# Four-layer graph network: the norm through PSUM, a deeper lookahead, and GpSimd's sums as eight pointer-scalar adds

## The chip, the cores and the metric

The kernel runs on one core of a Trainium2 chip. Its engines are TensorE (PE in the profile; PEld is its weight load), VectorE (DVE), ScalarE (ACT), GpSimd (POOL) and SyncE (SP). The metric is the device time of one execution, in microseconds.

## The reference

The input x holds 64 graphs of 256 nodes with 128 features, and adj is one 256x256 matrix. Four layers follow each other; each adds the output of a graph layer to x, and each begins with a layer norm over the features and a Relu:

```python
h = jnp.maximum(_layernorm(x, axis=-1), 0.0)
x = x + layer(h, adj, weights)
```

Layer 0 is a gated recurrent unit of five steps (two sigmoids and a tanh on products of h and adj @ h). Layer 1 is a polynomial in adj with a Relu. Layer 2 is (adj + I) @ h through one weight, normalised to length one. Layer 3 is an attention whose score takes a leaky Relu of every pair of nodes:

```python
pre = s1[:, :, None, :] + s2[:, None, :, :] + b_lin   # (graph, i, j, 256 channels)
h = jnp.where(pre >= 0, pre, ALPHA * pre)
e = jnp.einsum('bije,e->bij', h, a) + bias
out = sigmoid(softmax(e, axis=2) @ x)
```

This last score is nearly all of the work: 64 graphs x 256 x 256 pairs x 256 channels.

## The kernel before

Work goes by pairs of graphs (NB = 2, 32 pairs). For a pair, `front(p)` (lines 314 to 446) computes layers 0 to 2 and the inputs of layer 3's score; it is a generator that hands control back at each `yield`, 85 pieces in all (STEPS_OF_FRONT). The score of a pair goes in 64 slots: slot n stands for a node block `ic` (two of 128 nodes) and a row r (32), and covers rows r, r+32, r+64 and r+96 of the block for both graphs. Each slot has two tiles of 128 partitions (channels) by 4 x 2 x 256 = 2048 values, one for each half of the channels:

- the first half, `rl_v` (L515), is one VectorE maximum of 128x2048 that reads `s2a` from PSUM and `s1n` from SBUF, both broadcast;
- the second half goes two ways. Of every three slots, two have GpSimd make the sum `rl_g` (L504 in `make_sum`: one broadcast tensor_tensor add of `s2b` and `s1b`, 128x2048, all in SBUF), and ScalarE then applies the Relu in place (L518). The third slot has ScalarE do sum and Relu at once in eight instructions of 128x256, with a column of `s1b` as the per-partition bias (L524, `rl_s`).

`scores(n)` (L527 to 536) then has TensorE multiply both tiles by a 128x32 window of weights, four row groups each, into the PSUM tile `pe`. After 32 slots a `tail` (L450 to 483) takes a block's scores through softmax, two matmuls and a tanh to the output; its last two GpSimd instructions are L480 (times 0.5 plus 0.5, 128x256) and L481.

The main loop (L567 to 583) writes out the order of the work. For slot n it issues make_sum(n + SUM_AHEAD), make(n + AHEAD), then some pieces of the front of the next pair and of the one after it (`advance`, by a count of yields), then on odd slots a piece of a tail, then scores(n). `in_order()` ties every instruction of TensorE, VectorE, ScalarE and GpSimd to the one before it on its engine, so each engine runs in exactly this program order. AHEAD is 2 and SUM_AHEAD 5; `rl_v` has 3 buffers, `rl_g` 4, `rl_s` 2. All short-lived PSUM tiles of fronts and tails rotate through five banks (`bank`).

A front calls `norm` (L236 to 255) four times: statistics on VectorE (L243, L245); `inverse_root` on GpSimd (L233 adds the epsilon, L234 raises to the power -0.5; it also serves layer 2's normalisation, on `rn`); then four VectorE tensor_scalar operations of 128x128 that subtract the mean and multiply, from SBUF into the SBUF tile `h` (L250); then GpSimd's maximum with zero over all of `h`, 128x512 (L254). The transposes of h by TensorE follow (L262), or products with adj (L278). L417, the layer 2 result, is a group of four VectorE operations of 128x128 that read PSUM and SBUF and write SBUF.

Of the kernel before, what the change touches and what calls it, by code (L numbers as in the profile page):

```python
# [14 lines left out]
P = 128  # L15
NB = 2
# [2 lines left out]
NORM_EPS = 1e-12  # L19
ALPHA = 0.2  # L20
ENGINES = (mybir.EngineType.PE, mybir.EngineType.DVE, mybir.EngineType.Activation, mybir.EngineType.Pool)
AHEAD = 2
SUM_AHEAD = 5
SLOTS = 64


# [1 line left out]
def kernel(  # L28
# [207 lines left out]
    def norm(src, h):  # L236

        stats = work.tile([P, NB * NC, 6], F32, name="stats")
        mv = work.tile([P, NB * NC, 2], F32, name="mv")
        s = src.rearrange("p b c d -> p (b c) d")  # L240
        hh = h.rearrange("p b c d -> p (b c) d")
        for k in range(NB * NC):
            nc.vector.bn_stats(stats[:, k, :], s[:, k, :])  # L243
        for k in range(NB * NC):
            nc.vector.bn_aggr(mv[:, k, :], stats[:, k, :])  # L245
        yield
        inverse_root(mv[:, :, 1], OP.add, LN_EPS)
        yield
        for k in range(NB * NC):
            nc.vector.tensor_scalar(hh[:, k, :], s[:, k, :], mv[:, k, 0:1], mv[:, k, 1:2],  # L250
                                    op0=OP.subtract, op1=OP.mult)
        yield
        hh = h.rearrange("p b c d -> p (b c d)")
        nc.gpsimd.tensor_scalar(hh, hh, 0.0, None, op0=OP.max)  # L254
        yield

    def to_feature(h, name):

# [42 lines left out]
    def feat(name, **kw):  # L301
        return work.tile([P, NB, N], F32, name=name, **kw)

    def tok(name, **kw):
        return work.tile([P, NB, NC, D], F32, name=name, **kw)

    def add_row(po, row):

        t = po.rearrange("p b c d -> p (b c) d")
        nc.vector.tensor_add(t, t, row.unsqueeze(1).to_broadcast([P, NB * NC, D]))  # L310
# [3 lines left out]
    def front(p):  # L314
# [1 line left out]
        x0 = XIN.pop(p)  # L316


        h = tok("h", bufs=3)
        yield from norm(x0, h)  # L320
        pt = to_feature(h, "pt")
        pm = mix_nodes(h, adj_t, "pm")
        yield
        hT = feat("hT", bufs=4)
        nc.scalar.copy(hT, pt)
        mT = feat("mT", bufs=3)
        nc.scalar.copy(mT, pm)
        yield
        for step in range(STEPS):
            if step:  # L330
                pm = mix_nodes(h, adj_t, "pm")
                yield
                mT = feat("mT", bufs=3)
                nc.scalar.copy(mT, pm)
                yield
            pr = project(bank([P, NB, N], "pr"), [(u3t, hT), (w4t, mT)])
            yield
            r = bank([P, NB, N], "r")
            nc.scalar.activation(r, pr, AF.Tanh, bias=br, scale=0.5)
            yield  # L340
            rh = feat("rh")
            nc.vector.scalar_tensor_tensor(rh, r, 1.0, hT, op0=OP.add, op1=OP.mult)
            project(pr, [(w34, mT)], start=False)
            yield
            nc.scalar.activation(pr, pr, AF.Tanh, bias=bz, scale=0.5)
            pv = project(bank([P, NB, N], "pv"), [(w5t, mT), (u5t, rh)])
            yield
            nc.scalar.activation(pv, pv, AF.Tanh, bias=bh, scale=1.0)  # L348
            yield

            d = feat("d")
            nc.vector.tensor_sub(d, pv, hT)
            nc.vector.scalar_tensor_tensor(pr, pr, 1.0, d, op0=OP.add, op1=OP.mult)  # L353
            hT_new = feat("hT", bufs=4)
            nc.vector.scalar_tensor_tensor(hT_new, pr, 0.5, hT, op0=OP.mult, op1=OP.add)  # L355
            hT = hT_new
            yield
            pt = to_token(hT, "pt")
            yield
            if step < STEPS - 1:  # L360
                h = tok("h", bufs=3)
                nc.scalar.copy(h, pt)  # L362
                yield
        x1 = tok("x1")
        nc.vector.tensor_add(x1, x0, pt)


        h = tok("h", bufs=3)
        yield from norm(x1, h)
        pt = to_feature(h, "pt")  # L370
        pm = mix_nodes(h, adj_n, "pm")
        yield
        hT = feat("hT", bufs=4)
        nc.scalar.copy(hT, pt)
        c1T = feat("c1T")
        nc.scalar.copy(c1T, pm)
        yield
        pt = to_token(c1T, "pt")
        yield
        c1 = tok("c1", bufs=1)  # L380
        nc.scalar.copy(c1, pt)
        yield
        pm = mix_nodes(c1, adj_n, "pm")
        yield
        c2T = feat("c2T", bufs=1)
        nc.vector.scalar_tensor_tensor(c2T, pm, 2.0, hT, op0=OP.mult, op1=OP.subtract)
        yield
        po = project_token([(hT, th[:, 0, :]), (c1T, th[:, 1, :]), (c2T, th[:, 2, :])], "po")
        yield
        add_row(po, bias1)  # L390
        x2 = tok("x2")
        nc.vector.scalar_tensor_tensor(x2, po, 0.0, x1, op0=OP.max, op1=OP.add)


        h = tok("h", bufs=3)
        yield from norm(x2, h)
        pm = mix_nodes(h, adj_ti, "pm")
        yield
        yT = feat("yT", bufs=1)
        nc.scalar.copy(yT, pm)  # L400
        yield
        po = project_token([(yT, w2)], "po")
        yield
        add_row(po, bias2)
        yield
        sq = tok("sq", bufs=1)
        nc.scalar.square(sq, po)
        yield
        rn = work.tile([P, NB * NC], F32, name="rn")
        nc.vector.tensor_reduce(rn, sq.rearrange("p b c d -> p (b c) d"), AX.X, OP.add)  # L410
        yield
        inverse_root(rn, OP.max, NORM_EPS * NORM_EPS)
        yield
        x3 = tok("x3")
        for b in range(NB):
            for c in range(NC):
# [4 lines left out]
        h3 = tok("h3")  # L421
        yield from norm(x3, h3)
        pt = to_feature(h3, "pt")
        yield
        hT = feat("hT3")
        nc.scalar.copy(hT, pt)
        yield
        p1 = project(bank([P, NB, N], "p1"), [(adj_t[:, 0, P:2 * P], hT)])
        p2 = project(bank([P, NB, N], "p2"), [(adj_t[:, 1, P:2 * P], hT)])
        yield  # L430
        s2b = feat("s2b")
        nc.scalar.copy(s2b, p2)
        s1b = feat("s1b")
# [2 lines left out]
        for k in range(NB * NC):  # L436
            b, c = divmod(k, NC)
            nc.tensor.matmul(pc[:, k:k + 1], hT[:, b, c * P:(c + 1) * P], g1, start=True, stop=True)
        yield
        crow = work.tile([P, NB * NC], F32, name="crow")  # L440
        nc.vector.tensor_scalar(crow, pc, c_b, None, op0=OP.add)
        p1 = project(bank([P, NB, N], "p1"), [(adj_t[:, 0, 0:P], hT)])
        yield
        s1n = feat("s1n")
        nc.scalar.activation(s1n, p1, AF.Identity, bias=nblin[:, 0:1], scale=-1.0)
        READY[p] = [x3, h3, hT, crow, s1n, s1b, None, s2b]

    STEPS_OF_FRONT = 85

    def tail(p, ic, pe, x3, h3, crow):  # L450

        t = work.tile([P, NB, N], F32, name="sc")
        for b in range(NB):
            nc.vector.scalar_tensor_tensor(t[:, b, :], pe[:, b, :], crow[:, b * NC + ic:b * NC + ic + 1], adj_n[:, ic, :],
                                           op0=OP.add, op1=OP.add)
# [9 lines left out]
        nc.vector.reciprocal(rs, sums)  # L465
        pt = to_token(t, "pt")
        yield
        wT = work.tile([P, NB, NC, P], F32, name="wT")
        nc.scalar.mul(wT, pt, 0.5)
        yield  # L470
        po = bank([P, NB, D], "po")
# [27 lines left out]
    def make_sum(n):  # L499
        if n >= NPAIR * SLOTS or n % 3 == 0:  # L500
            return
        ops = READY[where(n)[0]]
        TILES[n, 1] = relu_pool.tile([P, 4, NB, N], F32, name="rl_g", bufs=4)
        nc.gpsimd.tensor_add(TILES[n, 1], *operands(n, ops[5], ops[7]))  # L504

    def make(n):
        if n >= NPAIR * SLOTS:
            return
        p, ic, r = where(n)
        ops = READY[p]  # L510
        if ops[6] is None:
            ops[6] = ps_s.tile([P, NB, N], F32, name="s2a")
            project(ops[6], [(adj_t[:, 1, 0:P], ops[2])])
        TILES[n, 0] = relu_pool.tile([P, 4, NB, N], F32, name="rl_v", bufs=3)
        nc.vector.tensor_tensor(TILES[n, 0], *operands(n, ops[4], ops[6]), op=OP.max)  # L515
        if n % 3:
            t = TILES[n, 1].rearrange("p g b n -> p (g b n)")
            nc.scalar.activation(t, t, AF.Relu)  # L518
        else:
            TILES[n, 1] = relu_pool.tile([P, 4, NB, N], F32, name="rl_s", bufs=2)  # L520
            for g in range(4):
                for b in range(NB):
                    i = ic * P + g * 32 + r
                    nc.scalar.activation(TILES[n, 1][:, g, b, :], ops[7][:, b, :], AF.Relu,  # L524
                                         bias=ops[5][:, b, i:i + 1], scale=1.0)
# [13 lines left out]
    PE = [None]  # L539
    FRONTS = {}  # L540

    def advance(p, upto):

        if p >= NPAIR:
            return
        if p not in FRONTS:
            load_x(p + 1)
            FRONTS[p] = [front(p), 0]
        f = FRONTS[p]
        while f[1] < upto and p not in READY:  # L550
            next(f[0], None)
            f[1] += 1
            in_order()

    in_order()
    half = STEPS_OF_FRONT // 2
    for k in range(STEPS_OF_FRONT + 8):
        advance(0, k)
        advance(1, k * half // STEPS_OF_FRONT)
    for n in range(SUM_AHEAD):  # L560
        make_sum(n)
    for n in range(AHEAD):
# [4 lines left out]
    for n in range(NPAIR * SLOTS):  # L567
# [2 lines left out]
        make(n + AHEAD)  # L570
        in_order()
        k = min(n % SLOTS + 1, room)
        advance(p + 1, 10 ** 6 if k == room else half + k * (STEPS_OF_FRONT - half) // room)
        advance(p + 2, (n % SLOTS + 1) * half // SLOTS)
        if tails and n % 2:
            if next(tails[0], 0) == 0:
                tails.pop(0)
# [40 lines left out]
```

## Time and profile before

| | us |
|---|---|
| median of 3 runs | 6881.86 (6881.08 to 6882.07) |
| the profiled execution | 6881.12 |
| its span | 6879.3 |
| a pair of graphs in the steady state | about 210 |
| granted TensorE clock, mean | 0.933 |

A line of the groups of instructions reads: source line, engine, operation, output and inputs, shapes, count, then busy time in us and mean duration of one in ns, then the engine's idle time just before these instructions and what ended most of it. A line of a timeline reads: start, length, engine, source line, operation, operands, number of instructions, and in brackets the idle time before and what ended it. A tile's view gives the shortest, median and longest duration in ns, then the first and the last start. Durations of VectorE and ScalarE instructions overlap a little when they follow each other, so a group's time is less than count times duration.

### The profile page before, as it was taken

Reading aid. Unit: us, or ns where it says so; the run is one execution under the profiler, and the core shown is the slowest. Engines: PE = TensorE matmul, PEld = TensorE weight load, DVE = VectorE, ACT = ScalarE, POOL = GpSimd, SP = SyncE. Lnnn points to the kernel's source line nnn. Section 1 sums busy time; section 2 is a strip of 40 time slices with the busy share of each in tenths; the row PEclk is TensorE's granted clock in tenths of the full one; section 3 lists DMA queues with packets and bytes.
Section 4 is the critical chain, followed back from the end, with each engine's and each line's share of the span. In section 5 each row is a group of like instructions: output and inputs, shape, how many; then the busy total and the mean of one; then the engine's idle time right before and its main releaser. Section 6 shows DMA issues by size and latency. Waiting matters only on the chain.

```text
span 6879.3 us, 98866 instructions
## 1 busy us (share of the span) xinstructions
PE 5854.8 (85%) x40021; PEld 2128.4 (31%) x40021; DVE 6045.8 (88%) x4868; ACT 5442.0 (79%) x8366; POOL 5381.2 (78%) x1947
## 2 busy tenths in 40 slices
PE   6888888888888888888898888888888988888888
PEld 3333233322323333333233333233332333233222
DVE  3988998889889888988898888988889988888898
ACT  3787887878878787877887788877877877788789
POOL 2777787778878777877787788877877877787799
PEclk8999999999999999999999999999999999999999
DMA  0000000000000000000000000000000000000000
GB/s 14 3 3 4 4 2 4 3 4 4 2 4 4 3 4 2 4 4 3 4 4 2 4 3 4 4 2 4 3 4 4 2 4 4 3 2 2 2 3 3
DMA packets 38651, 24.43 MB, mean 4 GB/s; under 512 B 3504, under 2 KB 38192, under 8 KB 38192
## 3 DMA queue, kind: packets, MB, share of 16 engines
q1 hardware_dynamic: 35088, 17.05, 0.9%
q8 instruction: 313, 5.13, 0.3%
q10 hardware_dynamic: 3104, 1.05, 0.1%
q14 instruction: 146, 1.20, 0.1%
HBM read 9.70 MB, written 8.39 MB: 3 GB/s over the span
## 4 chain that ended last, share of the span: by engine, by line
PE 50%; DVE 27%; POOL 12%; issue 7%; ACT 4%; DMA 0%; ACTq 0%; POOLq 0%; DVEq 0%; SPq 0%
PE pe L536 29%; DVE rl_v L515 13%; POOL rl_g L504 9%; DVE h L250 7%; PE pm L278 7%; PE pr L287 5%; PE pv L287 3%; PE pt L270 2%; PE po L297 2%; ACT rl_s L524 2%; POOL h L254 1%; PE p L287 1%; ACT rl_g L518 1%; DVE pr L353 1%; DVE hT L355 1%
## 5 line engine op out<-in xcount | busy, mean ns | idle before, releaser
L504 POOL TENSOR_TENSOR rl_g<-s2b,s1b 128x2048 f32<-128x2048 f32 x1365 | 4922.1, 3622 | 1230.3 <-PE pe L536 1013.1
L515 DVE TENSOR_TENSOR rl_v<-s2a,s1n 128x2048 f32<-128x2048 f32 x2048 | 4598.2, 2282 | 638.6 <-PE pe L536 586.0
L518 ACT ACTIVATE rl_g<-rl_g 128x2048 f32<-128x2048 f32 x1365 | 2590.7, 1907 | 390.8 <-POOL rl_g L504 387.7
L536 PE MATMUL pe<-rl_v,win 128*32 128x512 f32 x16384 | 2250.3, 620 | 52.2 <-DVE rl_v L515 50.5
L524 ACT ACTIVATE rl_s<-s2b,s1b 128x256 f32<-128x256 f32 x5464 | 2248.8, 498 | 0.0
L536 PE MATMUL pe<-rl_g,win 128*32 128x512 f32 x10920 | 1450.8, 604 | 3.0 <-ACT rl_g L518 3.0
L536 PEld LDWEIGHTS pe<-rl_v,win 128*32 128x32 f32 x16384 | 420.6, 112 | 1218.3 <-issue 781.3
L536 PE MATMUL pe<-rl_s,win 128*32 128x512 f32 x5464 | 741.2, 604 | 0.0
L536 PEld LDWEIGHTS pe<-rl_g,win 128*32 128x32 f32 x10920 | 357.8, 113 | 869.1 <-issue 746.6
L250 DVE TENSOR_SCALAR h<-x,mv 128x128 f32<-128x128 f32 x384 | 549.3, 1489 | 64.2 <-POOL mv L234 64.2
L270 PE MATMUL pt<-ident,hT 128*128 128x128 f32 x640 | 142.7, 364 | 407.6 <-DVE hT L355 407.6
L262 PE MATMUL pt<-ident,h 128*128 128x128 f32 x384 | 87.7, 369 | 351.3 <-POOL h L254 351.3
L278 PE MATMUL pm<-adj_t,h 128*128 128x256 f32 x1280 | 340.8, 414 | 3.5 <-ACT h L362 3.5
L536 PEld LDWEIGHTS pe<-rl_s,win 128*32 128x32 f32 x5464 | 183.9, 112 | 444.5 <-issue 377.1
L278 PEld LDWEIGHTS pm<-adj_t,h 128*128 128x128 f32 x1280 | 256.4, 209 | 103.8 <-issue 57.2
L254 POOL TENSOR_SCALAR h<-h 128x512 f32<-128x512 f32 x128 | 191.7, 1498 | 101.7 <-DVE h L250 101.7
L461 ACT ACTIVATE sc<-sc,nmx 128x256 f32<-128x256 f32 x128 | 64.0, 501 | 254.2 <-DVE nmx L457 254.2
L278 PE MATMUL pm<-adj_ti,h 128*128 128x256 f32 x256 | 112.8, 616 | 170.8 <-POOL h L254 170.8
L270 PEld LDWEIGHTS pt<-ident,hT 128*128 128x128 f32 x640 | 98.9, 186 | 513.7 <-DVE hT L355 394.9
L362 ACT COPY h<-pt 128x512 f32<-128x512 f32 x128 | 73.7, 576 | 198.2 <-PE pt L270 198.2
L348 ACT ACTIVATE pv<-pv,gate_b 128x512 f32<-128x512 f32 x160 | 104.3, 652 | 154.2 <-PE pv L287 154.2
L262 PEld LDWEIGHTS pt<-ident,h 128*128 128x128 f32 x384 | 56.1, 182 | 434.9 <-POOL h L254 409.2
(124 smaller groups left out, 4247.4 us busy)
## 6 DMA issues: line engine op xcount, KB each, us to landing
xin<-in_x_dram SPq DMA_DIRECT2D x64, 128.0 KB, 2.3
out_dram<-o SPq DMA_DIRECT2D x64, 128.0 KB, 1.8
w_raw<-in_L_gnn_w_w_dram ACTq DMA_DIRECT2D x3, 128.0 KB, 2.6
th_raw<-in_L_gnn_Theta_dram ACTq DMA_DIRECT2D x1, 320.0 KB, 3.2
adj_n<-in_adj_dram SPq DMA_DIRECT2D x1, 256.0 KB, 5.1
w_raw<-in_L_gnn_u_w_dram ACTq DMA_DIRECT2D x2, 64.0 KB, 2.3
bias<-in_L_gnn_bias_dram ACTq DMA_DIRECT2D x2, 64.0 KB, 3.5
w<-in_L_gnn_weight_dram ACTq DMA_DIRECT2D x1, 64.0 KB, 2.9
```

The lines of the kernel that those rows point to most:

```text
L250: nc.vector.tensor_scalar(hh[:, k, :], s[:, k, :], mv[:, k, 0:1], mv[:, k, 1:2], op0=OP.subtract, op1=OP.mult)
L254: nc.gpsimd.tensor_scalar(hh, hh, 0.0, None, op0=OP.max)
L262: nc.tensor.transpose(pt[:, b, c, :], h[:, b, c, :], ident)
L270: nc.tensor.transpose(pt[:, b, c, :], ht[:, b, c * P:(c + 1) * P], ident)
L278: nc.tensor.matmul(pm[:, b, :], h[:, b, c, :], a[:, c, :], start=(c == 0), stop=(c == NC - 1))
L287: nc.tensor.matmul(flat(pp), w, flat(t), start=start and k == 0, stop=stop and k == len(pairs) - 1, skip_group_check=True)
L297: nc.tensor.matmul(pp[:, b, c, :], t[:, b, c * P:(c + 1) * P], w, start=(k == 0), stop=(k == len(pairs) - 1))
L504: nc.gpsimd.tensor_add(TILES[n, 1], *operands(n, ops[5], ops[7]))
L515: nc.vector.tensor_tensor(TILES[n, 0], *operands(n, ops[4], ops[6]), op=OP.max)
L518: nc.scalar.activation(t, t, AF.Relu)
L524: nc.scalar.activation(TILES[n, 1][:, g, b, :], ops[7][:, b, :], AF.Relu, bias=ops[5][:, b, i:i + 1], scale=1.0)
L536: nc.tensor.matmul(flat(PE[0])[g * 32:(g + 1) * 32, :], win[:, k, 31 - r:63 - r], flat(rl[:, g]), start=False, stop=(r == 31 and k == NE - ...
```

## The change

It has three parts.

1. `norm` writes its four VectorE results into a PSUM tile `pn` instead of `h`, and ScalarE's Relu (L253 of the new kernel) takes that to `h` in SBUF. GpSimd's maximum is gone.
2. AHEAD goes from 2 to 4 and SUM_AHEAD from 5 to 7; `rl_v` gets 5 buffers and `rl_g` 6. The short-lived SBUF tiles of fronts and tails, which had their own buffers, share one ring of 14 ("short"). Each `yield` of a front carries a weight, and `advance` goes by the sum of weights (122 in all) instead of a count; the step that updates the state (`d`, then `pr` and `hT`) is split in two by a yield.
3. GpSimd's sum is eight tensor_scalar adds of 128x256, each with a column of `s1b` as a per-partition scalar, instead of one broadcast tensor_tensor.

```diff
-AHEAD = 2
-SUM_AHEAD = 5
+AHEAD = 4
+SUM_AHEAD = 7
...
-        yield
+        yield 1.6
         inverse_root(mv[:, :, 1], OP.add, LN_EPS)
-        yield
+        yield 0.4
+        pn = bank([P, NB * NC, D], "pn")
         for k in range(NB * NC):
-            nc.vector.tensor_scalar(hh[:, k, :], s[:, k, :], mv[:, k, 0:1], mv[:, k, 1:2],
+            nc.vector.tensor_scalar(pn[:, k, :], s[:, k, :], mv[:, k, 0:1], mv[:, k, 1:2],
                                     op0=OP.subtract, op1=OP.mult)
-        yield
-        hh = h.rearrange("p b c d -> p (b c d)")
-        nc.gpsimd.tensor_scalar(hh, hh, 0.0, None, op0=OP.max)
-        yield
+        yield 1.6
+        nc.scalar.activation(h.rearrange("p b c d -> p (b c) d"), pn, AF.Relu)
+        yield 1.0
...
+    SHORT = dict(tag="short", bufs=14)
...
-        h = tok("h", bufs=3)
+        h = tok("h", **SHORT)
...
             nc.vector.tensor_sub(d, pv, hT)
+            yield 1.1
             nc.vector.scalar_tensor_tensor(pr, pr, 1.0, d, op0=OP.add, op1=OP.mult)
...
-        TILES[n, 1] = relu_pool.tile([P, 4, NB, N], F32, name="rl_g", bufs=4)
-        nc.gpsimd.tensor_add(TILES[n, 1], *operands(n, ops[5], ops[7]))
+        TILES[n, 1] = relu_pool.tile([P, 4, NB, N], F32, name="rl_g", bufs=6)
+        _, ic, r = where(n)
+        for g in range(4):
+            for b in range(NB):
+                i = ic * P + g * 32 + r
+                nc.gpsimd.tensor_scalar(TILES[n, 1][:, g, b, :], ops[7][:, b, :], ops[5][:, b, i:i + 1], None, op0=OP.add)
...
-        TILES[n, 0] = relu_pool.tile([P, 4, NB, N], F32, name="rl_v", bufs=3)
+        TILES[n, 0] = relu_pool.tile([P, 4, NB, N], F32, name="rl_v", bufs=5)
...
-        while f[1] < upto and p not in READY:
-            next(f[0], None)
-            f[1] += 1
+        while f[1] < share * WORK and p not in READY:
+            f[1] += next(f[0], 0.0)
             in_order()
...
-        advance(p + 1, 10 ** 6 if k == room else half + k * (STEPS_OF_FRONT - half) // room)
-        advance(p + 2, (n % SLOTS + 1) * half // SLOTS)
+        advance(p + 1, 2.0 if k == room else 0.5 + 0.5 * k / room)
+        advance(p + 2, 0.5 * (n % SLOTS + 1) / SLOTS)
```

## The prediction

> **What bounds the kernel now.** I read the busy table first, then the chain of work that ended last, then the costliest groups.
>
> ```profile
> PE 5854.8 (85%) x40021; PEld 2128.4 (31%) x40021; DVE 6045.8 (88%) x4868; ACT 5442.0 (79%) x8366; POOL 5381.2 (78%) x1947
> PE 50%; DVE 27%; POOL 12%; issue 7%; ACT 4%; DMA 0%; ACTq 0%; POOLq 0%; DVEq 0%; SPq 0%
> ...
> L504 POOL TENSOR_TENSOR rl_g<-s2b,s1b 128x2048 f32<-128x2048 f32 x1365 | 4922.1, 3622 | 1230.3 <-PE pe L536 1013.1
> L515 DVE TENSOR_TENSOR rl_v<-s2a,s1n 128x2048 f32<-128x2048 f32 x2048 | 4598.2, 2282 | 638.6 <-PE pe L536 586.0
> ...
> L250 DVE TENSOR_SCALAR h<-x,mv 128x128 f32<-128x128 f32 x384 | 549.3, 1489 | 64.2 <-POOL mv L234 64.2
> ```
>
> See three things. No engine is full: VectorE is fullest (6045.8 of 6879.3 us), the others are close behind, and the chain changes engines all the time. GpSimd has slack: of its 1230.3 us of idle time before sums, 1013.1 end with TensorE freeing a buffer. And one row is out of proportion: the norm's `h` at L250 takes 1489 ns for 128x128, where the 128x2048 maximum takes 2282.
>
> The timelines of VectorE and GpSimd say why. First the start of the kernel, when GpSimd makes no sums, then the steady state:
>
> ```profile
> 25.59 1.11 DVE L250 TENSOR_SCALAR h<-xin,mv 128x128 f32<-128x128 f32 x4 [1.49 <-POOL mv L234]
> ...
> 3072.32 1.12 DVE L417 SCALAR_TENSOR_TENSOR x<-po,rn,x 128x128 f32<-128x128 f32 x4
> ...
> 3080.04 7.72 DVE L250 TENSOR_SCALAR h<-x,mv 128x128 f32<-128x128 f32 x4 [1.16 <-POOL mv L234]
> ```
> ```profile
> 3079.97 7.19 POOL L504 TENSOR_TENSOR rl_g<-s2b,s1b 128x2048 f32<-128x2048 f32 x2
> 3087.85 1.50 POOL L254 TENSOR_SCALAR h<-h 128x512 f32<-128x512 f32 x1 [0.68 <-DVE h L250]
> ```
>
> Four L250 cost 1.11 us alone and 7.72 us while two sums run. They are held until GpSimd's sums end. L417, with one operand in PSUM, never is: 335 to 351 ns in all 128, with GpSimd busy 78% of the time. So what blocks is an SBUF-to-SBUF operation of VectorE beside a GpSimd sum. Everything behind it in VectorE's order then waits: TensorE idled 8.55 us before the transposes of this h.
>
> **The norm through PSUM.** L250 has 512 instructions, 549.3 + 136.4 = 685.7 us. With the output in PSUM I take L417's group of four, 1.12 us: 128 x 1.12 = 143 us. No row reads SBUF alone and writes PSUM; the bounds are the bn_stats group (0.86 us for four: 110 us) and L417's full duration (4 x 0.342: 175 us). Saving: **543 us** of VectorE, 511 to 576. In the chain's full list L250 holds 7.5%, 516 us, so nearly all of it is on the path.
>
> GpSimd's L254 goes (128 x 1.50 = 192 us busy; 1.4% of the chain, 96 us). In its place ScalarE gets 128 Relus 128x512 from PSUM, by the copies of that shape (0.57 us) 73 us, on an engine that was busy 5442 us; they stand where L254 stood in the dependency. Net on the path: 96 - 73 = **23 us** saved, between -73 and 192. The 64 us that VectorE waited for GpSimd's power I leave as they are. Each norm takes one more of the five rotating PSUM banks, for about 1.6 units of front work, which is under two steps of the loop; no wait for a bank shows in the profile as a cost, so zero to R2's price below.
>
> **Deeper lookahead.** AHEAD goes from 2 to 4 and rl_v from 3 to 5 buffers, so make(n+AHEAD) still waits for scores(n-1): VectorE's 586.0 us of waiting for TensorE are tied to the same slot as before. What it can give is TensorE's wait for rl_v, 371.4 us by the waits view, when four tiles instead of two are ready. I take a quarter, **100 us**, between 0 and 371. The same holds for sums (5 to 7, buffers 4 to 6). The new yield weights put the norm two rl_v tiles behind its statistics in most cases, where it was three: less cover for GpSimd's power. The shared "short" ring moves no work; no price.
>
> **GpSimd's sums.** 1365 sums of 3622 ns become 10,920 adds of 128x256 with a per-partition scalar. The trace has no such add. The tile views give the nearest rows:
>
> ```profile
> L480 POOL TENSOR_SCALAR o<-o x64: 407/407/417, 312.6 to 6875.1; 128x256 f32<-128x256 f32 x64
> ```
> ```profile
> L254 POOL TENSOR_SCALAR h<-h x128: 1497/1498/1500, 26.8 to 6682.1; 128x512 f32<-128x512 f32 x128
> ```
> ```profile
> L233 POOL TENSOR_SCALAR mv<-mv x128: 223/228/237, 24.2 to 6672.9; 128x4 f32<-128x4 f32 x128
> L233 POOL TENSOR_SCALAR rn<-rn x32: 224/224/226, 133.3 to 6663.0; 128x4 f32<-128x4 f32 x32
> ```
>
> L480 (multiply and add, constants) has the exact shape: 8 x 0.407 = 3.26 us. L254 (a maximum, so another operation, but one-operation like the new add) is far dearer per element: half of it is 749 ns, 8 x 0.749 = 5.99 us; a line through L233's 225 ns at 4 elements and 1498 at 512 gives 857 ns at 256, 6.85 us. So a sum costs **3.26 to 6.85 us** against 3.61 now (start to start). I take 0.45 us an add, L480 and a tenth for fetching the scalar: 3.6 us, no change. The choice goes by shape and by arithmetic; the two L233 rows, add and maximum, cost the same at 4 elements, which says nothing of the slope. At 3.6 us GpSimd's total is 1365 x 3.6 + 276 (L233, L234, L480, L481) = 5190 us and stays below the others.
>
> The Trainium skill's page "GPSIMD Engine Reference" speaks on both sides. Section 4.1 (Engine selection) calls one-input operations roughly line-rate, which L480 fits and L254, at 2.9 ns an element, does not. Section 7 (Performance pitfalls) charges about 102 cycles for each small read command that does not overlap the one before; if each scalar were one, at that page's 1.2 GHz, that would be about 85 ns, an estimate: 8 x (0.407 + 0.085) = 3.94 us a sum, where the row alone gives 3.26. No row here shows that fetch.
>
> **The sum.** 6881 (the profiled execution: span 6879.3 and 1.8 around it; the median of the runs shown is 6881.9, the same) - 543 - 23 - 100 + 0 = 6215. A second way: from 2999 to 3192 us VectorE's timeline has three L250 groups, and a fourth begins at its end; outside of them it makes 60 rl_v tiles in 174.7 us, 2.91 us each. 64 x 2.91 + 4 x 1.12 = 191 us a pair, x 32 = 6112, + 159 for the start and end (6879 - 32 x 210, the present pair): 6271, with nothing from the lookahead. I say **6220**.
>
> What is late next: all four. VectorE 6046 - 543 = 5503, ScalarE 5442 + 73 = 5515, GpSimd 5190, TensorE 5855 at most. TensorE's own floor: 64 x 1.75 us (8 scores records at a pitch of 0.87, twice) plus about 65 us of other matmuls (62 records of 128x512 at 0.48 us, 64 of 128x256 at 0.24, some 20 us for the rest and the switches; counts from the rows, pitches from the chain) is 177 us a pair, x 32 + 159 = 5823. If the add is as L480 and lookahead gives all its 371 us: 6881 - 576 - 96 - 371 = 5838; I put the low end at 5900. If the add costs 0.5 us (4.0 a sum, GpSimd 5736) and the lookahead gives nothing, about 6400. The forecast's own range is **5900 to 6400**.
>
> **Rivals.**
>
> R1, slower: the add costs as L254, and GpSimd becomes the bound. Its work is then 1365 x 8 x (add) + 276, begun at 149 us (first sum in the trace) and with 14 us behind the last: at 0.749 us 8179 + 276 + 163 = 8618; at 0.857 us 9358 + 439 = 9797. It decides from (6881 - 439) / 10,920 = 0.59 us an add. For it: L254, and two L233 rows alike. Against: L480, same shape and engine, one operation more and 0.407.
>
> R2, smaller gain: a wait takes the place of the one removed. The power sits in GpSimd's order behind a sum, and VectorE's norm now stands a tile closer to it or waits for its PSUM bank. If each of 128 norms waited for one sum, 128 x 3.6 = 461 us instead of 67.5: 6220 + 393 = 6613. An add of 0.50 to 0.58 ends there too. For it: the 1.16 us in brackets above. Against: only 36 such waits before.
>
> R3, it doesn't do what it says: VectorE is held by GpSimd with a PSUM output also. But then a piece of 0.41 us, not 3.62, is waited for: at worst 512 x (0.28 + 0.41) = 353 us, 210 over 143: 6410. Counted with R2.
>
> **Chances.** Forecast 0.50 (0.02 of it under 5900). R2, R3 and dear-but-bearable adds (6400 to 6867) 0.10. Within 0.2% 0.02. R1 0.38, of which 0.22 from 6896 to 8700 (adds to half of L254) and 0.16 above. The range 5900 to 8700 holds 0.48 + 0.10 + 0.02 + 0.22 = 0.82; the far end, 9797, is left out with that 0.16. Faster 0.60, same 0.02, slower 0.38; 0.2% is about what a measurement of this kernel tells from no change.
>
> **What would show it.** The new add's duration decides most: 0.41 to 0.50 right, over 0.59 R1, with "POOL rl_g" leading the chain and ScalarE waiting for it. The norm is right if its four pieces take about 1.1 us and L250 leaves the chain; R2 shows as "DVE pn" waiting for "POOL mv" or for ScalarE. Lookahead: TensorE's 371 us for rl_v fall. Wrong altogether if the adds are cheap and the span still stays above 6600: then some order between the engines that I don't price holds them.

## The result, and the profile after

| | before | after |
|---|---|---|
| median, us | 6881.76 (6881.08 to 6882.07, 4 runs) | 10283.24 (10282.86 to 10283.69, 4 runs) |
| span of the profiled execution, us | 6879.3 | 10281.4 |
| granted TensorE clock, mean | 0.933 | 0.808 |

The changed kernel takes 1.494 times as long (95% interval 1.492 to 1.497). It is slower, and lies above the top of the range (8700). It is the rival R1, with a dearer add than the range reached to.

These are the busy table, the chain that ended last, and three groups of the changed kernel.

```profile
PE 6527.1 (63%) x40021; PEld 2324.9 (23%) x40021; DVE 5605.4 (55%) x4868; ACT 5544.2 (54%) x8494; POOL 10095.5 (98%) x11374
...
POOL 86%; issue 8%; PE 4%; ACT 1%; DVE 1%; DMA 0%; ACTq 0%; POOLq 0%; SPq 0%; DVEq 0%
...
L510 POOL TENSOR_SCALAR rl_g<-s2b,s1b 128x256 f32<-128x256 f32 x10920 | 9823.6, 922 | 9.7 <-ACT s1b L436 9.7
...
L524 ACT ACTIVATE rl_g<-rl_g 128x2048 f32<-128x2048 f32 x1365 | 2605.9, 1910 | 3747.9 <-POOL rl_g L510 3747.7
...
L250 DVE TENSOR_SCALAR pn<-x,mv 128x128 f32<-128x128 f32 x384 | 159.0, 414 | 1263.5 <-POOL mv L234 1253.1
```

Read them from the idle times. Once begun, GpSimd never waits before a sum again (9.7 us in all, at the start), and ScalarE waits 3747.7 us for GpSimd. One engine is full and all others wait for it. An add takes 922 ns, and 9823.6 / 10,920 = 0.900 us from one to the next, so a sum costs 7.20 us instead of 3.61. R1's own formula with that number gives 10,920 x 0.900 + 276 + 163 = 10,267.

The last row holds the other half of the story. The norm's VectorE work did get cheap: 159.0 us for 384, where it was 549.3. It now waits for GpSimd's power instead, which stands behind a queue of adds.

### The profile page after: what moved, and what is told of

It reads as the page before. It is cut to its first block, busy times and chain, and to the rows that moved or that the text cites. A ratio compares the mean times of both kernels' runs of the same rounds, so it can differ in the third digit from the quotient of the medians.

```text
span 10281.4 us, 108211 instructions
## 1 busy us (share of the span) xinstructions
PE 6527.1 (63%) x40021; PEld 2324.9 (23%) x40021; DVE 5605.4 (55%) x4868; ACT 5544.2 (54%) x8494; POOL 10095.5 (98%) x11374
## 4 chain that ended last, share of the span: by engine, by line
POOL 86%; issue 8%; PE 4%; ACT 1%; DVE 1%; DMA 0%; ACTq 0%; POOLq 0%; SPq 0%; DVEq 0%
POOL rl_g L510 84%; PE pe L542 2%; PE pm L277 1%; POOL mv L234 1%; PE pr L286 0%; POOL o L483 0%; PE pv L286 0%; ACT rl_g L524 0%; POOL mv L233 0%; DVE pn L250 0%; POOL o L482 0%; POOL rn L234 0%; ACT rl_s L530 0%; PE pt L269 0%; PE pt L261 0%
## 5 line engine op out<-in xcount | busy, mean ns | idle before, releaser
L510 POOL TENSOR_SCALAR rl_g<-s2b,s1b 128x256 f32<-128x256 f32 x10920 | 9823.6, 922 | 9.7 <-ACT s1b L436 9.7
L524 ACT ACTIVATE rl_g<-rl_g 128x2048 f32<-128x2048 f32 x1365 | 2605.9, 1910 | 3747.9 <-POOL rl_g L510 3747.7
L542 PE MATMUL pe<-rl_v,win 128*32 128x512 f32 x16384 | 2459.8, 676 | 1.9 <-DVE rl_v L521 1.9
L542 PE MATMUL pe<-rl_g,win 128*32 128x512 f32 x10920 | 1528.7, 634 | 114.0 <-ACT rl_g L524 114.0
L250 DVE TENSOR_SCALAR pn<-x,mv 128x128 f32<-128x128 f32 x384 | 159.0, 414 | 1263.5 <-POOL mv L234 1253.1
L277 PE MATMUL pm<-adj_t,h 128*128 128x256 f32 x1280 | 433.0, 498 | 335.8 <-ACT h L364 335.8
L286 PE MATMUL pr<-mT,w 128*128 128x512 f32 x320 | 257.7, 899 | 457.4 <-ACT r L340 457.4
L253 ACT ACTIVATE h<-pn 128x512 f32<-128x512 f32 x128 | 76.4, 597 | 792.8 <-DVE pn L250 792.8
L286 PE MATMUL pv<-rh,u5t 128*128 128x512 f32 x320 | 195.0, 695 | 402.1 <-DVE rh L343 402.1
L286 PE MATMUL pr<-mT,w4t 128*128 128x512 f32 x320 | 211.6, 749 | 275.9 <-ACT mT L335 275.6
L353 DVE TENSOR_TENSOR d<-pv,hT 128x512 f32<-128x512 f32 x160 | 110.1, 688 | 473.5 <-ACT pv L349 473.5
```

What stands on the lines that cost most here:

```text
L250: nc.vector.tensor_scalar(pn[:, k, :], s[:, k, :], mv[:, k, 0:1], mv[:, k, 1:2], op0=OP.subtract, op1=OP.mult)
L277: nc.tensor.matmul(pm[:, b, :], h[:, b, c, :], a[:, c, :], start=(c == 0), stop=(c == NC - 1))
L286: nc.tensor.matmul(flat(pp), w, flat(t), start=start and k == 0, stop=stop and k == len(pairs) - 1, skip_group_check=True)
L510: nc.gpsimd.tensor_scalar(TILES[n, 1][:, g, b, :], ops[7][:, b, :], ops[5][:, b, i:i + 1], None, op0=OP.add)
L542: nc.tensor.matmul(flat(PE[0])[g * 32:(g + 1) * 32, :], win[:, k, 31 - r:63 - r], flat(rl[:, g]), start=False, stop=(r == 31 and k == NE - ...
```

## The experiments

A time with a range in brackets is a median of four runs, any other is one run. Beside each, the kernel before ran on the same chip (6875.8 to 6882.0 us in all). Three dots in a code cut or a profile stand for lines left out.

**The third part undone, and done alone.** e1 is the changed kernel with the old broadcast sum:

```diff
-        _, ic, r = where(n)
-        for g in range(4):
-            for b in range(NB):
-                i = ic * P + g * 32 + r
-                nc.gpsimd.tensor_scalar(TILES[n, 1][:, g, b, :], ops[7][:, b, :], ops[5][:, b, i:i + 1], None, op0=OP.add)
+        nc.gpsimd.tensor_add(TILES[n, 1], *operands(n, ops[5], ops[7]))
```

> The changed kernel with its third part undone: GpSimd's sums are one broadcast tensor_tensor again (six buffers kept). Theory (all of the loss is the price of the new add; the norm and the lookahead gain what the prediction's terms say): 5900 to 6400 us, about 6220, L250 groups of about 1.1 to 1.7 us for four, VectorE near 5500 us busy. Rival (the norm through PSUM or the new order costs time too, and the adds hide it): 6880 us or more, with VectorE or TensorE waiting for GpSimd's power or for a PSUM bank.

Measured: 6597.4 us (6594.6 to 6597.5), 0.959 of the kernel before (0.957 to 0.960). Neither theory holds. The first two parts do gain, 283 us, but less than half of what was forecast, though VectorE's busy time (5573.3 us) fell by 473 of the 543 us forecast. So a second question opens: where did that time go?

e2 puts the eight adds into the kernel before, and nothing else.

> The kernel before with the third part alone: eight pointer-scalar adds for each sum, four buffers, the old norm and lookahead. Theory (GpSimd is the bound and nothing else counts): 10,920 adds at a pitch of 0.900 us are 9828 us; with GpSimd's other 468 us (276 and the 192 of L254) and 163 at the ends about 10,460 us, some 180 above the changed kernel. Rival (the other two parts cost time beside the adds): clearly under 10,283 us.

Measured: 10,686.3 us. GpSimd is the bound as expected; the 226 us above the estimate are about its waits before the adds (231.1, with the shallow lookahead and four buffers), by this group of e2:

```profile
L508 POOL TENSOR_SCALAR rl_g<-s2b,s1b 128x256 f32<-128x256 f32 x10920 | 9831.0, 920 | 231.1 <-PE pe L540 150.0 <-ACT rl_g L522 65.1 <-ACT s1b L434 8.3
```

The add costs the same 0.900 us beside the old norm and beside the new, so it isn't contention with the norm that makes it dear.

**Why the add costs 0.9 us.** e3 runs a list of GpSimd instructions before the fronts, each like these two:

```diff
+        nc.gpsimd.tensor_scalar(md[:, k * 256:(k + 1) * 256], ma[:, 0:256], sc0, None, op0=OP.add)
...
+        nc.gpsimd.tensor_scalar(md[:, k * 256:(k + 1) * 256], ma[:, 0:256], 1.0, sc0, op0=OP.mult, op1=OP.add)
```

> The kernel before with a list of GpSimd instructions ahead of its fronts, four of each kind, whose results nobody reads: one-operation adds with a constant and with a per-partition scalar (64, 256 and 1024 columns), maximum, multiply, multiply-and-add with constants, with one and with two per-partition scalars, and broadcast tensor_tensor. Only their durations count. Theory A (fetching the scalar is dear): the add with a constant takes about 0.41 us at 256 columns and the one with a scalar about 0.5 us more at any width. Theory B (the one-operation form is dear per element, as the maximum): the add with a constant takes about 0.9 us at 256 as well, and multiply-and-add stays near 0.41 to 0.5 us also with a scalar. Theory C (a scalar operand slows every element): the add with a scalar takes about 0.9 us at 256 and about 3.4 us at 1024, with a constant 0.41 and about 1.1, and multiply-and-add with a scalar is dear too.

The view of e3's tile that they write, with shortest, median and longest duration in ns. A column is the per-partition scalar. In order: add with a constant and with a column (256 elements a partition), with a column at 64 and at 1024, with a constant at 1024; maximum and multiply (256); multiply-and-add with constants at 256 and 1024, with one column and with two (256); add with a column, then maximum (256); and the broadcast tensor_tensor add at 256 and 1024.

```profile
L560 POOL TENSOR_SCALAR md<-ma x4: 847/852/866, 2.3 to 4.8; 128x256 f32<-128x256 f32 x4
L562 POOL TENSOR_SCALAR md<-ma,acol x4: 915/954/1117, 18.9 to 21.8; 128x256 f32<-128x256 f32 x4
L564 POOL TENSOR_SCALAR md<-ma,acol x4: 435/436/436, 22.7 to 24.0; 128x64 f32<-128x64 f32 x4
L566 POOL TENSOR_SCALAR md<-ma,acol x4: 2842/2842/2842, 24.5 to 33.3; 128x1024 f32<-128x1024 f32 x4
L568 POOL TENSOR_SCALAR md<-ma x4: 2767/2768/2768, 36.2 to 44.8; 128x1024 f32<-128x1024 f32 x4
L570 POOL TENSOR_SCALAR md<-ma x4: 843/843/848, 47.6 to 50.1; 128x256 f32<-128x256 f32 x4
L572 POOL TENSOR_SCALAR md<-ma x4: 847/847/853, 50.9 to 53.3; 128x256 f32<-128x256 f32 x4
L574 POOL TENSOR_SCALAR md<-ma x4: 404/404/405, 54.1 to 55.2; 128x256 f32<-128x256 f32 x4
L576 POOL TENSOR_SCALAR md<-ma x4: 1044/1044/1044, 55.7 to 59.1; 128x1024 f32<-128x1024 f32 x4
L578 POOL TENSOR_SCALAR md<-ma,acol x4: 478/478/479, 60.3 to 61.7; 128x256 f32<-128x256 f32 x4
L580 POOL TENSOR_SCALAR md<-ma,acol x4: 554/554/555, 62.1 to 63.7; 128x256 f32<-128x256 f32 x4
L582 POOL TENSOR_SCALAR md<-ma,acol x4: 1134/1138/1144, 64.3 to 67.6; 128x256 f32<-128x256 f32 x4
L584 POOL TENSOR_TENSOR md<-ma,acol x4: 611/612/612, 68.7 to 70.4; 128x256 f32<-128x256 f32 x4
L586 POOL TENSOR_TENSOR md<-ma,acol x4: 1892/1892/1892, 71.1 to 77.0; 128x1024 f32<-128x1024 f32 x4
```

Theory B holds. The single add has the maximum's price, 852 and 843 ns at 256 columns, and 2.49 ns an element ((2768 - 852) / 768). Multiply-and-add, with one operation more, takes 0.83 ns an element ((1044 - 404) / 768). A column instead of a constant adds a fixed 74 ns (2842 - 2768, and 478 - 404 in the other form), nothing per element; only the four single adds at 256 scatter, from 915 to 1117. Two operations are not what helps: add and then maximum takes 1138. Of the tensor_scalar forms tried only multiply-and-add is fast; why, no run shows.

e4 writes the same sums in that form:

```diff
-                nc.gpsimd.tensor_scalar(TILES[n, 1][:, g, b, :], ops[7][:, b, :], ops[5][:, b, i:i + 1], None, op0=OP.add)
+                nc.gpsimd.tensor_scalar(TILES[n, 1][:, g, b, :], ops[7][:, b, :], 1.0, ops[5][:, b, i:i + 1],
+                                        op0=OP.mult, op1=OP.add)
```

> The changed kernel with each add written as two operations: times 1.0, then plus the per-partition scalar. The sums are the same numbers. Theory B (the one-operation form is dear): each takes about 0.41 to 0.5 us, GpSimd is no longer the bound, and the time is 5900 to 6400 us. Theories A and C (the scalar is what costs): 0.9 us each as now or more, about 10,280 us.

Measured: 6574.7 us, each add 479 ns. A factor of 1.0 takes away 3708 of the 10,283 us. It misses 5900 to 6400 by the same shortfall as e1.

**Where the first two parts' gain went.** In e1 and in e4 GpSimd, VectorE and ScalarE wait most for TensorE to give their buffers back. Here is a stretch of e4 on TensorE, VectorE and ScalarE:

```profile
4018.06 1.04 PE L543 MATMUL pe<-rl_g,win 128*32 128x512 f32 x8
4022.53 0.65 PE L261 MATMUL pt<-ident,h 128*128 128x128 f32 x4 [3.43 <-ACT h L253]
4023.03 1.89 PE L277 MATMUL pm<-adj_t,h 128*128 128x256 f32 x8
```
```profile
4017.90 2.28 DVE L522 TENSOR_TENSOR rl_v<-s2a,s1n 128x2048 f32<-128x2048 f32 x1
4020.10 1.75 DVE L250 TENSOR_SCALAR pn<-xin,mv 128x128 f32<-128x128 f32 x4
```
```profile
4012.76 3.72 ACT L525 ACTIVATE rl_g<-rl_g 128x2048 f32<-128x2048 f32 x2
4021.88 0.60 ACT L253 ACTIVATE h<-pn 128x512 f32<-128x512 f32 x1 [5.41 <-DVE pn L250]
```

TensorE stands still for 3.43 us in front of transposes that need h, though two rl_v tiles for later slots lie ready and a third is being made (VectorE has begun 1223, TensorE has used 1220); it can't pass the transposes. The norm that owes h stands on VectorE behind that third tile. Tiles in store don't help where a front's piece is late. From this came theory L, and four kernels. e5 is the kernel before with the norm alone; e6 is e1 with its front paced by equal steps; e7 is e1 with the old depth; e8 is e4 with the old depth but the new buffers:

```diff
e6
-            f[1] += next(f[0], 0.0)
+            next(f[0], None)
+            f[1] += WORK / 90
e8
-AHEAD = 4
-SUM_AHEAD = 7
+AHEAD = 2
+SUM_AHEAD = 5
```

> The kernel before with the first part alone: the norm's four results go to a PSUM tile, ScalarE's Relu takes them to SBUF; old lookahead, old yields, broadcast sums. The prediction's terms give 6881 - 473 (measured saving of VectorE's busy time in the changed norm) - 23 = about 6385 if VectorE's time is the span's time. Theory L (TensorE stops in its program order at a front's piece that VectorE or ScalarE owes it, and they stand at a tile of their own; the tiles it has ready do not help): 6550 to 6700, like the norm with everything else (6597). Rival D (the deeper lookahead costs time and the norm alone gains all): 6400 or less.

> The changed kernel with broadcast sums (6597) but its front paced by a count of yields again (90 equal steps) instead of by weights. If the weights matter, 1 to 3 per cent slower than 6597; theory L says that how evenly TensorE's pieces lie matters little: 6570 to 6700.

> The changed kernel with broadcast sums (6597) but the old lookahead: AHEAD 2, SUM_AHEAD 5, rl_v 3 and rl_g 4 buffers. Theory L: the depth gives nothing, since make(n+AHEAD) waits for scores(n-1) in both: 6540 to 6660. Rival D (depth costs, by the 506 us that ScalarE newly waits for rl_s buffers): 6500 or less. The prediction's term (lookahead saves 100 us): about 6700.

> The changed kernel with multiply-and-add sums (6575), AHEAD 2 and SUM_AHEAD 5, but with the five rl_v and six rl_g buffers kept. make(n+2) then waits for scores(n-3), so VectorE and GpSimd may run two slots ahead of TensorE and reach a front's piece early. Theory L: VectorE's waits for TensorE and TensorE's waits for fronts both fall, 6250 to 6450. Rival P (TensorE's own work, 88% busy, is the bound): within 1% of 6575.

Measured: e5 6319.1, e6 6330.1, e7 6571.1, e8 6048.5 us.

The norm alone gains 560 us, twice what the first two parts gain together. Theory L missed that one and e6, and named too small a gain for e8. The depth gives nothing: old against new is 6571 to 6597 with weights, and e6, with the new depth, is no better than e5 without; as e6 also has the shared ring and the split step, these two do no visible harm either. Rival D met e5's number, but e7 refutes it: depth is not what costs. What costs is the weights, 267 us (6597 to 6330). And e8 shows the lockstep: with buffers that let VectorE run two slots ahead of TensorE, VectorE's wait for them falls from 749.2 to 82.2 us and 526 us go. The smaller AHEAD by itself is not the reason, since e7 has it too, without spare buffers and with broadcast sums. Whether it is the spare rl_v or the spare rl_g buffers no run parts. These are the waits of e4 and then of e8 (total, times, longest):

```profile
POOL rl_g L510 <- PE pe L543: 854.3, 411, 7.3
DVE rl_v L522 <- PE pe L543: 749.2, 543, 3.6
...
ACT rl_s L531 <- PE pe L543: 453.5, 276, 4.7
PE pt L269 <- DVE hT L357: 444.5, 127, 8.8
```
```profile
POOL rl_g L510 <- PE pe L543: 242.7, 166, 4.6
...
PE pt L269 <- DVE hT L357: 175.9, 97, 3.9
...
DVE rl_v L522 <- PE pe L543: 82.2, 78, 2.0
```

Rival P falls too: TensorE's own work was not the floor at 6575.

**The weights.** Three kernels followed. e10 is e1 with no weight under 1.3 (and the total, WORK, raised to 140.6 to match); e11 is e1 with the old norm, that is the second part alone; e9 is e8 with equal steps, as in e6:

```diff
e10
-            f[1] += next(f[0], 0.0)
+            f[1] += max(next(f[0], 0.0), 1.3)
e11
-            nc.vector.tensor_scalar(pn[:, k, :], s[:, k, :], mv[:, k, 0:1], mv[:, k, 1:2],
+            nc.vector.tensor_scalar(hh[:, k, :], s[:, k, :], mv[:, k, 0:1], mv[:, k, 1:2],
...
-        nc.scalar.activation(h.rearrange("p b c d -> p (b c) d"), pn, AF.Relu)
+        nc.gpsimd.tensor_scalar(hh, hh, 0.0, None, op0=OP.max)
```

> Multiply-and-add sums, AHEAD 2 and SUM_AHEAD 5 with the five rl_v and six rl_g buffers (6048 with weights), and the front paced by a count of yields. If what the weights cost (267 us of 6597) is lost in the same way here: about 5800 to 5900. If free buffers already cover it (VectorE ahead of TensorE, so that a front's piece is there when TensorE comes to it): 5980 to 6080.

> The changed kernel with broadcast sums (6597), its weights kept but none under 1.3 (total 140.6 instead of 122), so that no two dependent pieces of a front fall into one slot; counting the program's own order, five such pairs in each front do so with the weights as they are, and none with equal steps. Theory G (those pairs are what the weights cost: TensorE stands still for the whole way through VectorE, GpSimd and ScalarE): 6320 to 6420. Rival H (it is the uneven spacing of the other pieces): 6500 to 6620.

> The changed kernel with broadcast sums and the old norm (from SBUF to SBUF, GpSimd's maximum): the second part of the change alone. If the parts add up, the weights cost 250 to 270 us here too and the depth 0 to 30: 7100 to 7180. By the prediction's term (100 us saved): about 6780.

Measured: e9 6021.5 (6019.6 to 6026.2), ratio 0.8755 (0.874 to 0.877); e10 6259.9; e11 6707.5 us. With free buffers equal steps gain only 27 us (6048 to 6021, e9's second case), where they gained 267. e10 speaks for theory G and goes beyond it: with a floor, the weights are better than equal steps. e11 surprised: the second part alone gains 172 us. Its norm row says why. Compare L250 with the 1489 ns of before:

```profile
L250 DVE TENSOR_SCALAR h<-x,mv 128x128 f32<-128x128 f32 x384 | 193.8, 565 | 13.1 <-POOL mv L234 13.1
```

The 0.4 behind the power brings the norm close to it. By VectorE's timeline about half of the 128 norms then meet no sum (1.1 us for their four L250), and the others wait for the rest of one, 4.4 us at most; in the kernel before 5 norms were free and 102 took over 4 us. All L250 take 245 us here (193.8 and 51.0) where they took 686. So the second part removes the same stall as the first, by its order, and the gains don't add: VectorE's busy time falls by 432 us (6045.8 to 5613.5), the time by 172. The 260 us between are near the 267 that the weights cost e1; that it is the same cost is not shown, since no run has the old norm with equal steps.

e12 keeps the 0.4 behind the power and raises all other weights to at least 1.3 (WORK 136.1); e13 puts e10's floor on e8 (WORK 140.6):

```diff
e12
-            f[1] += max(next(f[0], 0.0), 1.3)
+            w = next(f[0], 0.0)
+            f[1] += w if w == 0.4 else max(w, 1.3)
e13
-            f[1] += next(f[0], 0.0)
+            f[1] += max(next(f[0], 0.0), 1.3)
```

> As the kernel with weights of at least 1.3 (6260), but the 0.4 behind GpSimd's power is kept (total 136.1): the four same-slot pairs that are left in a front are all power and then the VectorE work that needs it. If these pairs are what the weights cost: 6480 to 6600. If it is the others (transpose and copy, tanh and difference) or how evenly the rest lies: 6260 to 6350.

> Multiply-and-add sums, AHEAD 2 and SUM_AHEAD 5 with five rl_v and six rl_g buffers, weights of at least 1.3. With weights as they were this was 6048, with equal steps 6021. If the same-slot pairs still cost when VectorE may run ahead of TensorE: 5880 to 5980. If free buffers cover them: 6000 to 6060.

Measured: e12 6411.2, e13 5942.8 us (5913.5 to 5944.2), ratio 0.8625 (0.860 to 0.865). e12 lies between its two cases: the 0.4 costs 151 of the 337 us that the floor gains, the other short weights 186. Whether those 186 are same-slot pairs or the spacing in general stays open; no run parts them. With free buffers the floor still gains 106 us (6048 to 5943), as e13's first case had it. e13 is the fastest kernel of this study, with all engines near full:

```profile
PE 5638.9 (95%) x40021; PEld 2064.8 (35%) x40021; DVE 5513.6 (93%) x4868; ACT 5426.6 (91%) x8494; POOL 5310.3 (89%) x11374
```

## Why the prediction was wrong

**GpSimd's sums: the choice among the rows failed.** "I take 0.45 us an add, L480 and a tenth for fetching the scalar" went by shape; 0.900 us an add was measured. The right row was L254: as the prediction itself noted, it is one-operation like the new add. The line through L233 and L254 gave 857 ns; the add with a constant took 852. The two L233 rows, alike at 4 elements, were the hint that add and maximum share a price, and were put aside. L480 is multiply-and-add, and that form is the exception. The upper bound, 6.85 us a sum, lacked the scalar's 74 ns; the sum measured 7.20. The range left R1's far end out, and the time lies beyond even that end (9797), since its price per add was without the scalar: 10,920 x (0.900 - 0.857) = 470 of the 486 us between. (The scalar's 74 ns show as 43, mostly because the adds follow each other 22 ns sooner than their 922 ns and the line gave 857 where 852 was measured.)

**R1** was right in mechanism and formula: 10,267 by its sum, 10,283 measured. Its point of decision, 0.59 us an add, no run tests; the adds tried take 0.48 and 0.92.

**The norm: right, a little mis-sized.** 686 us became 212 (159.0 and 52.9), not 143: 414 ns each, above the upper bound taken from L417 (342). VectorE's busy time fell by 473 in e1, where 543 were forecast. R3 did not occur (and its sum is off: 6220 and 210 make 6430, not 6410): beside running sums all 512 lie between 403 and 417 ns. These are L250's durations in the kernel before, and in e1:

```profile
L250 DVE TENSOR_SCALAR h<-x,mv x384: 330/335/3657, 101.1 to 6681.7; 128x128 f32<-128x128 f32 x192
```
```profile
L250 DVE TENSOR_SCALAR pn<-x,mv x384: 403/414/417, 106.7 to 6401.3; 128x128 f32<-128x128 f32 x192
L250 DVE TENSOR_SCALAR pn<-xin,mv x128: 403/414/416, 25.4 to 6074.2; 128x128 f32<-128x128 f32 x128
```

Alone the norm gave 560 us of time (e5), where the prediction's two terms for it, 543 and 23, make 566. That the sum is so close is partly luck: VectorE's busy time fell by 480 in e5 (6045.8 to 5565.9), and 80 us more went, where 23 (between -73 and 192) were forecast. Where the 80 come from no run shows.

**The lookahead: a gain forecast, none found.** "I take a quarter, 100 us" measured as a loss of 26 with weights (e7 to e1). The wait that it was to be taken from did go: TensorE's 371.4 us for rl_v are 204.3 in e7 and 16.8 in e1. No time went with it. The reason was in the prediction, "make(n+AHEAD) still waits for scores(n-1)", and was not followed through: with buffers for AHEAD + 1 tiles no engine gets further ahead, whatever AHEAD is, and VectorE waits for TensorE instead (600.1 us in e7, 796.4 in e1). The prediction also says nothing of `rl_s`, which kept two buffers: 506 us of new waits for them came in e1, none in e7. At nearly equal times they cost little.

**The yield weights: no term at all.** The prediction saw "less cover for GpSimd's power" and priced it in R2 only. They cost 267 us with the new norm (e1 against e6). That e1's 6597 is close to R2's 6613 is chance: in e1 VectorE waited 13.7 us for the power in front of all its norms; R2 needed 461. What was late was the front's piece that TensorE needed next, as in the stretch of e4.

**The parts overlap.** Norm alone -560, second part alone -172, both -283. The prediction added terms; the first two cure the same stall, and the second brings a cost of its own.

**Two figures from a page.** The Trainium skill's page "GPSIMD Engine Reference", section 4.1 (Engine selection), calls one-input work roughly line-rate. That holds here for multiply-and-add (0.83 ns an element) and not for the single add (2.49) or the maximum. The estimate of 85 ns that the prediction worked out from that page's section 7 (Performance pitfalls), for a small read, is near the 74 measured for a scalar column; that the column is such a read, no run shows.

## What to carry to other kernels

Before an instruction is moved to another form, time that form in that engine: the nearest row is the one with the same operations, not the one with the same shape, and a list of fourteen forms cost some 50 us of one run. In a program order that ties several engines together, depth without spare buffers is no freedom; two buffers more than the lookahead asks for were worth 526 us here. And count how many slots lie between a piece and the piece that needs it: raising the shortest distances gained 337 us (e10), though how much of that is pairs in one slot is only partly known.

## What the hardware showed that was not expected

On GpSimd, an add of 128x256 is faster as a multiply by 1.0 and an add (404 ns with constants) than as an add alone (852). A broadcast tensor_tensor add, the kind that the change replaced, runs at 1.67 ns an element (612 ns at 256 columns, 1892 at 1024), between the two.

VectorE's L250 of 128x128 takes 414 ns from SBUF into PSUM, more than the same operation from SBUF to SBUF when no sum holds it (330), and more than L417, another operation, from PSUM and SBUF to SBUF (335 to 351).

The granted TensorE clock is higher where TensorE's busy share is higher: 0.808 at 63% busy (after), 0.933 at 85% (before), 0.967 at 91% (e5), 0.985 at 95% (e13). The order isn't strict: e6 has 0.974 at 90%. TensorE's score matmuls' records last longer at the low clock (676 ns in after, 620 before). No run here separates cause from effect. The Trainium skill's page "TensorE: Matmul & The Clock Gate", Part 1 (The HAM clock gate), says that the clock is held down by default and released by activity; the figures above agree with that direction.
